# Graph network on one core: masks of the adjacency search made from a bfloat16 copy that the row sums write

## The chip, the cores and the metric

The kernel runs on one core of a Trainium2 chip. The metric is the device time of one launch in microseconds (us), as the median of several runs. One further execution is recorded by the hardware profiler, and every view below is of that one. The engines are named as in the profile: PE is TensorE's matmul (PEld its weight loads), DVE is VectorE, ACT is ScalarE, POOL is GpSimd and SP is the engine that issues most of the DMAs. Each engine works through its own queue in the order of its instructions.

## What is computed

Four graph layers on 2708 nodes with 512 features each; after every layer the old features are added and the sum is normalized (LN). The adjacency matrix `adj` is 2708 x 2708 in float32 and mostly zero; an entry that isn't zero lies between 0.05 and 1.

```python
# layer 0
a = adj + eye;  d = 1 / sqrt(a.sum(axis=1))
x = LN(x + (d[:, None] * a * d[None, :]) @ x @ W0.T + b0)
# layer 1
head = (adj > 0) / max(sqrt(count of adj > 0 in the row), 1e-12);  inc = adj + head
x = LN(x + (inc @ x) / inc.sum(axis=1))
# layer 2: attention over the edges of adj, two gates, a sigmoid
x = LN(x + sigmoid(gate_a * (attn @ (x @ W_sa)) + gate_b * (adj @ (x @ W_g) + b_g)))
# layer 3: signs of x and of a weight
x = LN(x + relu(adj @ (max(sign(x), 0) @ sign(W3).T)))
```

What matters here is layer 0: it needs the sum of every row of `adj` (the degree), and the kernel uses the zeros of the matrix, so it first has to find where the other entries are.

## The kernel before

**The search.** The 2708 rows of `adj` are cut into 22 blocks of 128 (the last has 20). While the blocks stream in from memory, the kernel makes for each a list of the nodes that have an edge into it, so that later only the listed rows of features are gathered and only packed pieces of the matrix are multiplied. Blocks are taken in `GROUPS` of one to three (L55): (1,), (2, 3), (4, 5), (6, 7, 8) and so on up to (21,), and block 0, which is treated as dense, comes last. The order of arrival is in `arrival`.

**Turns.** `turn(at)` (L1242) writes out the work of one turn, and it is called for `at` = 0 to 25. The order is fixed by hand: `in_order` (L620) chains every instruction traced inside it to the one before it on the same engine, DMA issues included. Instructions from outside may be slotted in between by the scheduler. `each(action, k)` does an action for the k-th block to arrive; `chain(action, n)` does it for the group whose last block arrived n turns ago. The second group, called `SOON`, runs its whole chain in one turn, and so does the first group in turn 0.

**The steps that the change and the prediction touch:**

- `load` (L711) brings the block's rows as two halves, 1408 and 1300 columns wide, into buffers `arow`, of which there are four: two blocks. `load_x` brings the block's features and its piece of columns 0 to 127. SP issues both for the block two turns ahead.
- `sum_rows` (L805) is ScalarE's row sum: a copy of each half with an accumulated sum into `row_sums`. The copy itself goes to a buffer `unused` of one byte an element, and nothing reads it.
- `degree` (L813, DVE) adds the two half sums and 1. `root` (L824, ACT) takes the square root. `inverse_root` (L831) makes `dinv` from it by a reciprocal and a Newton step, four small DVE instructions that are placed between the masks.
- `mark` (L850) makes the mask of the block: per half a DVE comparison "not equal to 0" from `arow` into a bfloat16 tile (L874). For a block that lists its own diagonal tile apart, two short instructions follow on `arow` itself: the mask of the own 128 columns (L880) and a read of the diagonal (L886). They lie in the first half for blocks up to 10 and in the second from block 11. Between these stand the `others`: `own_diagonal` (L900) of the block before, `count` (L914) where a group has just become complete, and the four Newton steps. Then 22 small matmuls, `find` (L895), count the entries per node.
- The chain of a group: `count` (DVE) and `count_partitions` (PE) one turn after its last block, `steps_of` (a table on DVE, then the difference matmul L981) and `look_up` two turns after it, with ScalarE's copy `steps` (L990), comparisons on DVE and the `looked` matmuls; `keep_looked` (L1021) is ScalarE's copy of their result in the same turn. `list_nodes` (L1027), three turns after it, makes the list on DVE, and `fetch` (L1070) has POOL issue the indirect DMAs of the packed pieces.
- Feature work goes along: `transpose_x` (PE) for the block of this turn, `keep_transposed` (L1094, ACT) and `project0` (L1101, PE, four float32 matmuls of 512 columns) for the block before, `scale0` (L1111, ACT, with a DMA to `y_rows` from ScalarE's queue) for the one before that, and `fold` (DVE) and `grow0` (PE) for the one three turns back.

In a turn, ScalarE's queue so far has the order root of the block before, row sums of this block, `keep_transposed`, the copy `steps` where a group is at `look_up`, `scale0` with its DMA, and `keep_looked`.

Of the kernel before, what the change touches and what calls it, by code (L numbers as in the profile page):

```python
# [10 lines left out]
BF16 = mybir.dt.bfloat16  # L11
F16 = mybir.dt.float16
I32 = mybir.dt.int32
AF = mybir.ActivationFunctionType
ALU = mybir.AluOpType
# [4 lines left out]
P = 128  # L20
# [487 lines left out]
def sparse_layers(ctx, tc, x, adj, adj_t, w0_t, b0, w_sa, a_sa, w_gcnb, b_gcnb, wa, ba, wb, bb, w3_t,  # L508
# [19 lines left out]
    def rows(b: int) -> int:  # L528
        return min(P, N - b * P)

    def direct(b: int):

        return tuple(range(NB)) if b == 0 else DIRECT.get(b, ())
# [9 lines left out]
    f = [feat.tile([P, D], F32, tag=f"f{b}", name=f"f{b}") for b in range(NB)]  # L543
# [40 lines left out]
    def side_of(b: int):  # L584
        return sides[:, ways.index(SPLIT[b]), :]
# [22 lines left out]
    def own_by_itself(b: int) -> bool:  # L608
        return b not in direct(b)
# [88 lines left out]
    with tc.tile_pool(name="s_pre", bufs=1) as pre:  # L698
# [3 lines left out]
        NT = NB + 3  # L702

        CUT = (NB // 2) * P
        arows = {}
        row_sums = pre.tile([P, NB, 2], F32, name="s_row_sums")

        def place_of_x(b: int):
# [55 lines left out]
        turn_at, at = {}, 0  # L764
# [30 lines left out]
        near = pre.tile([P, KINDS - 1, NB], BF16, name="s_near")  # L795
# [8 lines left out]

        def sum_rows(b: int):  # L805
            m = rows(b)
            for h, ar in enumerate(arows[b]):
                unused = pre.tile([P, CUT], mybir.dt.uint8, tag="unused", name=f"unused{b}_{h}", bufs=1)
                nc.scalar.activation(  # L809
                    unused[:m, : ar.shape[1]], ar, AF.Copy, accum_out=row_sums[:m, b, h : h + 1]  # L810
                )

        def degree(b: int):  # L813

            m = rows(b)
            deg = small.tile([P, 1], F32, tag="deg", name=f"deg{b}")
            nc.vector.scalar_tensor_tensor(  # L817
                deg[:m], row_sums[:m, b, 0:1], 1.0, row_sums[:m, b, 1:2], op0=ALU.add, op1=ALU.add
            )
            degree_of[b] = deg  # L820
# [29 lines left out]
        def mark(b: int, others):  # L850

            others = iter(others)

            def other():
                next(others, lambda: None)()

            g = group_of[b]
            i = g.index(b)  # L860
            m = rows(b)
            if i == 0:
                find = ps_s.tile([P, D], F32, tag="find", name=f"find{b}", bufs=2)
                n = len(g)
                search[g] = {
                    "hits": find[:, : n * NB * KINDS].rearrange(
                        "p (g s c) -> p g s c", g=n, c=KINDS
                    ),
                    "before": find[:, D - n * KINDS :],
                    "diff": find[:, : n * NT * KINDS],  # L870
                }
            mask = masks[arrival.index(b) % 2]
            for ar, c0 in zip(arows[b], (0, CUT)):
                nc.vector.tensor_scalar(  # L874
                    mask[:m, c0 : c0 + ar.shape[1]], ar, 0.0, None, op0=ALU.not_equal
                )
                other()
                own = b * P - c0
                if own_by_itself(b) and 0 <= own < ar.shape[1]:
                    nc.vector.scalar_tensor_tensor(  # L880
                        mask[:m, b * P : b * P + m], ar[:, own : own + m], 0.0, off_dia[:m, :m],
                        op0=ALU.not_equal, op1=ALU.mult,
                    )
                    other()
                    scr = pre.tile([P, P], F32, tag="dia", name=f"dia{b}", bufs=1)
                    nc.vector.scalar_tensor_tensor(  # L886
                        scr[:m, :m], ar[:, own : own + m], 1.0, ident[:m, :m],
                        op0=ALU.mult, op1=ALU.mult, accum_out=dia[:m, b : b + 1],
                    )
            for j in direct(b):  # L890
                nc.vector.memset(mask[:m, j * P : (j + 1) * P], 0.0)  # L891
            for step_ in others:
                step_()
            for s in range(NB):
                nc.tensor.matmul(  # L895
                    search[g]["hits"][:, i, s, :], mask[:m, s * P : (s + 1) * P], side_of(b)[:m],
                    start=True, stop=True,
                )
# [339 lines left out]
        def each(action, at: int):  # L1238
            if 0 <= at < NTURN:
                action(arrival[at])  # L1240

        def turn(at: int):  # L1242
            step_of = {at - last_at[g]: g for g in GROUPS[1:]}

            def chain(action, since: int):
                if step_of.get(since, SOON) != SOON:
                    action(step_of[since])

            each(degree, at - 1)
            each(root, at - 1)  # L1250
            chain(steps_of, 2)
            each(sum_rows, at)
            each(keep_transposed, at - 1)
            steps = inverse_root(arrival[at - 1]) if 0 < at <= NTURN else []
            found_in = step_of.get(1)

            if found_in:
                steps.insert(0, lambda: count(found_in))
            if 0 < at <= NTURN:
                steps.insert(0, lambda: own_diagonal(arrival[at - 1]))  # L1260
            if at < NTURN and arrival[at]:
                mark(arrival[at], steps)
            else:
                for step_ in steps:
                    step_()
            if found_in:
                count_partitions(found_in)
                if found_in == SOON:
                    steps_of(SOON)
            each(load_x, at + 2)  # L1270
            each(load, at + 2)
            each(transpose_x, at)
            chain(look_up, 2)
            chain(list_nodes, 3)
            if found_in == SOON:
                look_up(SOON)
                keep_looked(SOON)
            if at == 0:
                for step_ in (
                    count, count_partitions, steps_of, look_up, keep_looked, list_nodes  # L1280
                ):
                    step_(GROUPS[0])
            each(scale0, at - 2)
            each(project0, at - 1)
            chain(keep_looked, 2)
            each(fold, at - 3)
            each(grow0, at - 3)
            if found_in == SOON:
                list_nodes(SOON)
            fetch(len(to_fetch))  # L1290
            if at == NTURN:
                count_block0()

        with in_order():
            for at in range(NTURN + 4):
                turn(at)
# [84 lines left out]
    with tc.tile_pool(name="s_l0", bufs=10, reuse_waits="tile") as lp:  # L1381
# [77 lines left out]
        for at, b in enumerate(sequence):  # L1459
            m = rows(b)  # L1460
# [108 lines left out]
    with tc.tile_pool(name="s_l1", bufs=8, reuse_waits="tile") as lp:  # L1569
# [67 lines left out]
        for at, b in enumerate(sequence):  # L1637
            m = rows(b)
# [348 lines left out]
    with tc.tile_pool(name="s_l3", bufs=11, reuse_waits="tile") as lp, \  # L1987
# [96 lines left out]
        for at, b in enumerate(order3):  # L2084
            m = rows(b)
# [120 lines left out]
```

## Time and profile before

| | |
|---|---|
| median of 3 runs | 1006.92 us (1006.87 to 1007.9) |
| the profiled execution | 1015.66 us, of which the span of its instructions is 1013.9 us |
| PE busy | 867.5 us (86% of the span) |
| DVE busy | 654.6 us (65%) |
| POOL busy | 513.0 us (51%) |
| ACT busy | 381.2 us (38%) |
| bytes moved | 220.06 MB, on average 217 GB/s |

Times inside the profile are counted from the start of the span. The search takes about the first 190 us of it; layers 0 to 3 fill the rest. The shares in the table are means over all of this, so for a change in the search they say little, and the slices and the timeline of that stretch have to be read. In a row of the groups by line, the numbers after the bar are the busy time in us and the mean of one instruction in ns, and then the engine's idle time before them with what ended it. In a row of the timeline the first number is the start, the second the duration, both in us, and the bracket holds the idle time before it and its releaser. In the list of waits the numbers are the total in us, how many, and the longest.

### The profile page before, as it was taken

Reading aid. Unit: us, or ns where it says so; the run is one execution under the profiler, and the core shown is the slowest. Engines: PE = TensorE matmul, PEld = TensorE weight load, DVE = VectorE, ACT = ScalarE, POOL = GpSimd, SP = SyncE. Lnnn points to the kernel's source line nnn. Section 1 sums busy time; section 2 is a strip of 40 time slices with the busy share of each in tenths; the row PEclk is TensorE's granted clock in tenths of the full one; section 3 lists DMA queues with packets and bytes.
Section 4 is the critical chain, followed back from the end, with each engine's and each line's share of the span. In section 5 each row is a group of like instructions: output and inputs, shape, how many; then the busy total and the mean of one; then the engine's idle time right before and its main releaser. Section 6 shows DMA issues by size and latency. Waiting matters only on the chain.

```text
span 1013.9 us, 12803 instructions
## 1 busy us (share of the span) xinstructions
PE 867.5 (86%) x3659; PEld 458.7 (45%) x3659; DVE 654.6 (65%) x2538; ACT 381.2 (38%) x822; POOL 513.0 (51%) x579
## 2 busy tenths in 40 slices
PE   1888889659587977989999988998999999699983
PEld 0444444212122324455555544453555555378762
DVE  5889797717366863546455436666888777556765
ACT  2665555100000012545445433333444333254654
POOL 2677888567666533646434034453454320066761
PEclk9898889879798988999999998999999999889986
DMA  9999895467676634766645266676786551299985
GB/s 288 332 330 313 293 299 162 142 197 215 189 228 202 199 122 132 216 198 207 199 150 165 80 235 239 225 272 219 261 320 224 176 176 44 82 308 331 310 233 169
DMA packets 93557, 220.06 MB, mean 217 GB/s; under 512 B 13660, under 2 KB 28364, under 8 KB 93476
## 3 DMA queue, kind: packets, MB, share of 16 engines
q0 software_dynamic: 43008, 127.61, 42.1%
q1 hardware_dynamic: 38520, 76.78, 22.3%
q10 hardware_dynamic: 11948, 14.76, 4.4%
q8 instruction: 31, 0.51, 0.2%
q14 instruction: 50, 0.41, 0.1%
HBM read 178.21 MB, written 31.71 MB: 207 GB/s over the span
## 4 chain that ended last, share of the span: by engine, by line
PE 63%; DVE 15%; issue 6%; DMA 6%; another core or an unknown queue 5%; ACT 3%; POOL 1%; ACTq 0%; DVEq 0%; SPq 0%; POOLq 0%
PE l L1369 11%; PE h L1595 7%; PE e L1820 6%; PE a L1820 6%; PE l L2075 4%; PE y L1106 4%; PE pg L1868 4%; PE l L2114 3%; PE pc L1868 3%; DMA xg<-x_rows,i 2%; PE e L1628 2%; PE px L1929 2%; PE a L1629 2%; DVE s_mask L874 1%
## 5 line engine op out<-in xcount | busy, mean ns | idle before, releaser
L613 POOL DMA_INDIRECT xg<-x_rows,i x98 | 94.8, 967 | 113.4 <-PE l L1369 65.7
L1072 POOL DMA_INDIRECT a<-in_adj_t_dram,row_at x98 | 111.0, 1132 | 59.2 <-DVE deg L817 24.0
L613 POOL DMA_INDIRECT xg<-y_rows,i x98 | 97.5, 995 | 50.3 <-issue 21.8
L1106 PE MATMUL y<-s_w,xt 128*128 128x512 f32 (+1 forms) x176 | 96.8, 702 | 0.0
L1369 PE MATMUL l<-xg,a 128*32 128x512 f32 (+3 forms) x196 | 83.2, 657 | 12.1 <-DMA xg<-y_rows,i 11.8
L613 POOL DMA_INDIRECT xg<-xw_rows,i x70 | 71.4, 1020 | 39.9 <-issue 16.5
L1796 POOL DMA_INDIRECT xg<-x_rows,i x60 | 59.9, 999 | 61.8 <-ACT ae L1551 18.0
L1595 PE MATMUL h<-s_wsa,xt 128*128 128x256 f32 (+3 forms) x352 | 83.5, 391 | 5.2 <-ACT xt L1590 5.0
L1796 POOL DMA_INDIRECT a<-x_rows,i x38 | 36.9, 970 | 93.3 <-DVE mask L1554 38.0
L1595 PEld LDWEIGHTS h<-s_wsa,xt 128*128 128x128 f32 (+1 forms) x352 | 65.4, 190 | 30.6 <-ACT xt L1590 14.0
L809 ACT ACTIVATE unused<-arow 128x1408 uint8<-128x1408 f32 (+3 forms) x44 | 58.3, 1325 | 2.4 <-DMA x_rows<-s_zero 1.7
L1106 PEld LDWEIGHTS y<-s_w,xt 128*128 128x128 f32 (+1 forms) x176 | 37.3, 223 | 43.4 <-issue 43.3
L2075 PE MATMUL l<-ws,pw 128*128 128x512 f32 (+1 forms) x210 | 52.0, 401 | 3.7 <-DVE pw L1999 3.7
L1820 PE MATMUL a<-xg,a 128*32 128x512 f32 (+2 forms) x120 | 50.9, 626 | 4.2 <-DMA xg<-x_rows,i 4.2
L1820 PE MATMUL e<-xg,ae 128*32 128x512 f32 (+2 forms) x120 | 47.9, 601 | 0.9 <-ACT ae L1556 0.9
L642 ACT ACTIVATE rsqs<-mv 128x1 f32<-128x1 f32 (+2 forms) x56 | 11.3, 201 | 94.8 <-DVE mv L671 48.9
L2075 PEld LDWEIGHTS l<-ws,pw 128*128 128x128 f32 (+1 forms) x210 | 40.4, 194 | 14.0 <-DVE pw L1999 4.6
L1868 PE MATMUL pg<-s_wg,pt 128*128 128x256 f32 (+1 forms) x176 | 44.9, 397 | 1.3 <-ACT pt L1856 1.3
L895 PE MATMUL find<-s_sides,s_mask 128*128 128x5 bf16 (+1 forms) x462 | 15.7, 166 | 34.8 <-DVE s_mask L891 25.0
L667 DVE BATCH_NORM_STATS2 st<-t 128x6 f32<-128x512 f32 (+1 forms) x66 | 45.3, 686 | 0.3
L1369 PEld LDWEIGHTS l<-xg,a 128*32 128x32 f32 (+3 forms) x196 | 19.6, 148 | 53.2 <-issue 33.0
L673 POOL TENSOR_TENSOR rs<-mv,s_neg_half 128x1 f32<-128x1 f32 (+1 forms) x22 | 12.9, 588 | 60.5 <-DVE mv L671 51.1
(306 smaller groups left out, 1965.6 us busy)
## 6 DMA issues: line engine op xcount, KB each, us to landing
arow<-in_adj_dram SPq DMA_DIRECT2D x21, 704.0 KB
arow<-in_adj_dram SPq DMA_DIRECT2D x21, 650.0 KB
x_rows<-f SPq DMA_DIRECT2D x40, 256.0 KB
aw<-in_adj_t_dram SPq DMA_DIRECT2D x21, 320.0 KB
y_rows<-yt ACTq DMA_DIRECT2D x20, 256.0 KB
x_rows<-h SPq DMA_DIRECT2D x19, 257.0 KB
f<-in_x_dram SPq DMA_DIRECT2D x19, 256.0 KB
h_own<-x_rows SPq DMA_DIRECT2D x19, 256.0 KB
```

The source lines that it names most:

```text
L613: nc.gpsimd.indirect_dma_start(out=t, out_offset=None, in_=src[:, :], in_offset=bass.IndirectOffsetOnAxis(ap=index[b][:, i : i + 1], axis=0),)
L667: nc.vector.bn_stats(st[:m], t[:m])
L809: nc.scalar.activation(unused[:m, : ar.shape[1]], ar, AF.Copy, accum_out=row_sums[:m, b, h : h + 1])
L1072: nc.gpsimd.indirect_dma_start(out=packed[b][:, t + len(direct(b)), :], out_offset=None, in_=adj_t, in_offset=bass.IndirectOffsetOnAxis(ap ...
L1106: nc.tensor.matmul(ps[:m], xt[:, k, :m], w0[:, k, :], start=(k == 0), stop=(k == KC - 1))
L1369: nc.tensor.matmul(ps[r0:r1], weights, moving, start=(i == order[0]), stop=last_of(b, i, order))
L1595: nc.tensor.matmul(ps, xt[:, k, :m], w[:, k, :], start=(k == 0), stop=(k == KC - 1))
L1796: nc.gpsimd.indirect_dma_start(out=g, out_offset=None, in_=x2_rows[:, :], in_offset=bass.IndirectOffsetOnAxis(ap=index[b][:, t : t + 1], a ...
L1820: nc.tensor.matmul(ps[r0:r1], weights, moving, start=(i == order[0]), stop=last_of(b, i, order))
L1868: nc.tensor.matmul(ps, pt[:, k, :m], w[:, k, :], start=(k == 0), stop=(k == KC - 1))
L2075: nc.tensor.matmul(whole[b], p[:r, h, b * P : (b + 1) * P], g[:r, :], start=(j == 0 and h == 0), stop=(j == NB - 1 and h == 1),)
L2114: nc.tensor.matmul(ps[:m], p[:, h, i * m : (i + 1) * m], src[i0 + i], start=False, stop=(i0 + i == len(src) - 1 and h == 1),)
```

## The change

The row sum writes its copy as bfloat16 into two buffers named `rough`, and the masks are made from these instead of from the float32 rows. For that the row sum of a block is moved from the turn of the block to the end of the turn before it; turn 0 does its own first. `degree` moves from the start of the next turn to the end of the block's own turn, and so does `root`, where it stands behind `keep_looked`. The own-diagonal instructions L880 and L886 still read the float32 rows.

```diff
-        arows = {}
+        arows, rough = {}, {}
...
         def sum_rows(b: int):
             m = rows(b)
+            rough[b] = []
             for h, ar in enumerate(arows[b]):
-                unused = pre.tile([P, CUT], mybir.dt.uint8, tag="unused", name=f"unused{b}_{h}", bufs=1)
+                near = pre.tile([P, CUT], BF16, tag="rough", name=f"rough{b}_{h}", bufs=2)
                 nc.scalar.activation(
-                    unused[:m, : ar.shape[1]], ar, AF.Copy, accum_out=row_sums[:m, b, h : h + 1]
-                )
+                    near[:m, : ar.shape[1]], ar, AF.Copy, accum_out=row_sums[:m, b, h : h + 1]
+                )
+                rough[b].append(near[:m, : ar.shape[1]])
...
             mask = masks[arrival.index(b) % 2]
-            for ar, c0 in zip(arows[b], (0, CUT)):
+            for ar, near, c0 in zip(arows[b], rough.pop(b), (0, CUT)):
                 nc.vector.tensor_scalar(
-                    mask[:m, c0 : c0 + ar.shape[1]], ar, 0.0, None, op0=ALU.not_equal
+                    mask[:m, c0 : c0 + ar.shape[1]], near, 0.0, None, op0=ALU.not_equal
                 )
...
-            each(degree, at - 1)
-            each(root, at - 1)
+            if at == 0:
+                each(sum_rows, 0)
             chain(steps_of, 2)
-            each(sum_rows, at)
             each(keep_transposed, at - 1)
...
             each(scale0, at - 2)
             each(project0, at - 1)
+            each(sum_rows, at + 1)
+            each(degree, at)
             chain(keep_looked, 2)
+            each(root, at)
             each(fold, at - 3)
```

## The prediction, made before the changed kernel had run

> **What bounds the kernel now.** The page's slices come first, to see which engines are full while adjacency rows are searched (0 to about 190 us of the span).
>
> ```profile
> DVE  5889797717366863546455436666888777556765
> ACT  2665555100000012545445433333444333254654
> DMA  9999895467676634766645266676786551299985
> ```
>
> One digit is 25.3 us. In slices 2 to 7 DVE is 70 to 90% busy, the DMA engines 80% and more, ScalarE only 50 to 60%: a change that takes work from DVE and gives ScalarE none looks safe. But the share does not say which wait ends last. The groups by line price the two operations concerned, and the list of waits shows what ScalarE idles for:
>
> ```profile
> L809 ACT ACTIVATE unused<-arow 128x1408 uint8<-128x1408 f32 x19 | 25.9, 1362 | 0.0
> L809 ACT ACTIVATE unused<-arow 128x1300 uint8<-128x1300 f32 x19 | 24.5, 1287 | 0.6
> ...
> L874 DVE TENSOR_SCALAR s_mask<-arow 128x1300 bf16<-128x1300 f32 x19 | 17.9, 944 | 0.0
> L874 DVE TENSOR_SCALAR s_mask<-arow 128x1408 bf16<-128x1408 f32 x19 | 17.8, 935 | 0.6 <-DMA arow<-in_adj_dram 0.6
> ...
> ACT steps L990 <- PE find L981: 22.0, 7, 4.9
> ```
>
> The last line decides my forecast: in seven turns ScalarE sits at the head of its queue waiting for a TensorE matmul, 22.0 us together, and whatever stands behind that waits too. The timeline of one cycle of three turns shows where:
>
> ```profile
> 84.30 0.32 PE L981 MATMUL find<-table,s_step 128*128 128x375 bf16 x1
> 84.66 0.47 ACT L990 CAST steps<-find 128x375 bf16<-128x375 f32 x1 [2.69 <-PE find L981]
> 85.03 0.69 ACT L1115 ACTIVATE yt<-y,s_dinv 128x512 f32<-128x512 f32 x1
> 85.75 0.33 ACTq L1116 DMA_DIRECT2D y_rows<-yt  x1
> 86.55 1.00 DVE L874 TENSOR_SCALAR s_mask<-arow 128x1408 bf16<-128x1408 f32 x1
> 87.72 0.83 DVE L874 TENSOR_SCALAR s_mask<-arow 128x1300 bf16<-128x1300 f32 x1
> 90.24 0.53 DVE L1038 TENSOR_TENSOR look<-look,turns 128x352 f32<-128x352 f32 x1
> 93.15 0.89 DVE L874 TENSOR_SCALAR s_mask<-arow 128x1408 bf16<-128x1408 f32 x1
> 99.19 0.43 PE L895 MATMUL find<-s_sides,s_mask 128*128 128x5 bf16 x10 [3.16 <-DVE s_mask L880]
> ```
>
> I call the turns of a group its count turn (count), look turn (steps copy L990) and list turn (list_nodes). Above: the look turn's difference matmul at 84.30, the list turn's masks at 86.55, listing from 90.24, the next count turn's masks from 93.15, and TensorE waiting until 99.19 for that turn's mask. From there TensorE needs 8.15 us (count_partitions, transposes, project0, grow0) to the next difference matmul at 107.34. So the ring is TensorE, then DVE; today DVE enters it without ScalarE, because masks are made straight from the rows.
>
> **What the Trainium skill says.** "VectorE: DVE Perf Modes", the section on the perf-mode tiers: a tensor_scalar from SBUF to SBUF goes at twice the base rate in float32 and four times in bfloat16; its 2048-element figures work out at 150 cycles plus elements over the factor, at 0.96 GHz. For 1408 and 1300 float32 elements that gives 0.89 and 0.83 us, just the undisturbed rows above; for bfloat16, as an estimate, 0.52 and 0.49. No bfloat16 mask is in this trace. "ScalarE: Activation LUTs", What ACT_TABLE_LOAD costs: an ACTIVATE with immediates takes 186 ns plus 0.833 ns per element, float32 and bfloat16 alike: 1.36 us for 1408, and the trace has 1362 ns. So I cost the change of output type on ScalarE at nothing (bounds 0 to 0.1 us). "TensorE: Matmul & The Clock Gate", Part 1: after an idle window the array runs at half clock until busy again; the trace agrees, with single L1106 matmul records from 592 to 1201 ns and a granted clock of 0.72 between 102 and 108 us.
>
> **The change part by part.** (1) Masks from bfloat16: DVE loses 0.94 + 0.94 - 1.01 = 0.87 us a turn, some 18 us over 21 turns. Not all of it is on the path.
>
> (2) The row sum one turn ahead. The mask of turn t+1 now waits for ScalarE's sum, and that stands at the end of turn t, behind the steps copy, scale0 and the y_rows DMA issue on the same queue; the listing copy L1024, the root and the next transposed copy stand behind it. In count and list turns this has cover: ScalarE reaches the sum several us before DVE asks. In the look turn it has none. From the difference matmul: 0.36 until the copy (84.66 - 84.30), 1.45 to the end of the DMA issue (86.1), two halves with their accumulator reads 2.97, a semaphore 0.1, second mask 0.49. The reciprocal then waits for the root, now behind the sum and L1024 (0.49 + 0.2 against the mask's 0.6): 0.3. The rest up to L1038, taken from 88.55 to 90.24 less a 0.35 wait for the sum that goes: 1.35. Together L1038 comes 7.0 us after the difference matmul. Difference starts in the five full cycles: 62.68, 84.30, 107.34, 131.81, 154.99; L1038 before: 68.16, 90.24, 113.94, 137.73, 160.16. So L1038 moves by +1.5, +1.1, +0.4, +1.1, +1.8. The following count turn's two masks get back (measured pair less 1.01) 0.96, 0.95, 1.23, 0.71, 0.67. Net +0.5, +0.1, -0.8, +0.4, +1.1: +1.3 us. The look turns' own saving is worth nothing: DVE then waits for ScalarE, about 2 us at the first mask. The early cycle with the count at 51.5 saves only its second mask, since own_diagonal waits for TensorE until 50.99: -0.4.
>
> (3) The start has no turn ahead. Before:
>
> ```profile
> 5.81 0.89 DVE L874 TENSOR_SCALAR s_mask<-arow 128x1408 bf16<-128x1408 f32 x1 [0.75 <-DMA arow<-in_adj_dram]
> ...
> 11.32 1.02 PE L895 MATMUL find<-s_sides,s_mask 128*128 128x5 bf16 x22 [11.32 <-DVE s_mask L891]
> ...
> 12.33 0.34 ACTq L744 DMA_DIRECT2D x_rows<-s_masked  x1
> ...
> 14.00 1.38 ACT L809 ACTIVATE unused<-arow 128x1408 uint8<-128x1408 f32 x1
> ```
>
> ScalarE issues zero fills until 12.7, loads a table until 14.0, and its halves end at 15.4 and 18.6 (16.9 if the second isn't again held by an interleaved weight load). So the first find moves from 11.3 to 17.6 or 19.2. Before, slack followed: DVE stood 2.92 us for the row sum, ScalarE 2.34 for a DMA. Running the same steps (find to base 4.0, base to look copy about 2.3) the look copy ends at 24.0 or 25.6, the next block's sum at 26.9 or 28.5. Now the root follows with its 1.28 us table load in the open (it ran at 22.0 in a wait before); reciprocal, diagonal and second mask take about 1.2, so the second find starts at 29.6 or 31.2 against 26.40: +3.2 to +4.8, I take +4.0. TensorE is back to back from there to the next find, so nothing absorbs it.
>
> (4) degree and root later: degree is small (0.15 us) and its sum is long done; the root's cost is in (2) and (3). Row buffers come free no later: the half without its own diagonal after the sum, the other after the diagonal read, and SP's x, column and direct-row loads keep their order. ScalarE needs a block earlier than DVE did, but loads are issued about 10 us before use (81.68 for the mask at 93.15) and in list turns the sum would start near 91: bound 0 to 1 us a cycle, taken as 0. The two rough buffers wait for the previous turn's masks, on the same DVE queue, before the sum is due. POOL's fetches shift with the lists: it idles 6.3 us before the last list (183.54), so its backlog doesn't hold it.
>
> **Sum.** +4.0 - 0.4 + 1.3 = about +5 us. Against the profiled execution (1015.66 us, its span 1013.9) that is 1020.6; on the median of 1006.92 it is 1012.
>
> **Rivals.** Faster: DVE is really the bound and the ring through ScalarE loosens. The three DVE turns 79.33 to 99.19 plus 2.3 to the base copy are 22.1 us; less 2.6 they are 19.5. If TensorE, idle less, kept its clock (project0 took 3.68 us for eight matmul records at full clock, 5.85 at 100.8), the 8.15 would shrink to 5.9 and the ring would gain about 2 us a cycle: -10 in five, with +4 at the start -6, so 1001. For: DVE is nearly without gaps from 60 to 107. Against: the wait of 3.16 at 99.19 stays, and with it the slow clock; and DMA, at 0.95 to 1.00 busy from 54 to 108, leaves little room.
>
> No change: the start's loss is half absorbed and the lists gain: 1007.
>
> Much slower: bfloat16 masks run no faster than float32 ones (+0.9 for each list and count turn, +9), or the sums wait for rows in the busy DMA stretches, 1 to 2 us in each cycle: 1018 to 1022. The first half of this is also the case that the change doesn't do what it says; the 16-bit comparisons of L1007 (284 ns for 256 elements, 348 for 512, 0.25 ns an element) speak against it.
>
> **How the numbers follow.** Chances: forecast 0.52, faster rival 0.20, no change 0.12, much slower 0.16. The forecast's own range is 1008 to 1017 (start 3.2 to 4.8, each cycle off by 0.7). For 8 in 10 I go from 1001 to 1020. About 2 us (0.2%) is what can be told from no change. Faster 0.20, within 0.13, slower 0.67.
>
> **What would show it.** Right: masks near 0.5 us; DVE idle at the first mask of list turns with ScalarE's sum as releaser; the first find after 17 us; find-to-difference times still near 8 us. Wrong: cycles under 21 us, or a first find before 14.

## The result, and the profile after

The changed kernel takes 1018.22 us (median of 22 runs, 1010.03 to 1023.26) against 1008.5 us for the kernel before beside it (22 runs). The ratio is 1.0079 with a 95% interval of 1.0056 to 1.0101: 5.6 to 10.2 us slower. The profiled execution took 1022.38 us, its span 1020.4 us. In the changed file the row sum stands one line further down (L809 is L810), what follows it two (L874 is L876, L1038 is L1040), and what follows `turn` up to four.

The slices of the changed kernel, one digit per 25.5 us:

```profile
DVE  4677578727445783555546427766888777555675
DMA  9899797376776625676655257786786551299984
```

DVE has become emptier in the search: slices 2 to 7 have 6 to 8, and one 5, where 7 to 9 stood. The DMA row changes by a tenth or two, both ways. The groups by line, shapes kept apart (busy time and mean ns of one, then the idle time before them by what ended it):

```profile
L810 ACT ACTIVATE rough<-arow 128x1408 bf16<-128x1408 f32 x21 | 28.9, 1377 | 8.4 <-ACT yt L1117 2.2 <-issue 2.1 <-DVE turns L1038 1.0
L876 DVE TENSOR_SCALAR s_mask<-rough 128x1408 bf16<-128x1408 bf16 x20 | 12.0, 598 | 26.2 <-ACT rough L810 16.6 <-issue 9.6
L876 DVE TENSOR_SCALAR s_mask<-rough 128x1300 bf16<-128x1300 bf16 x20 | 10.2, 511 | 2.0 <-ACT rough L810 2.0
```

The masks are as fast as hoped: 598 and 511 ns where 935 and 944 stood, and DVE's busy time fell from 654.6 to 638.2 us. The price is in the last column: 28.2 us of idle time ahead of the masks, 18.6 of them put down to ScalarE's sum; for the other 9.6 the profile names no releaser. The list of waits over the first 200 us has the same 18.6 us, and also what ScalarE itself waits for, TensorE's difference matmul:

```profile
ACT steps L992 <- PE find L983: 24.0, 6, 5.5
...
DVE s_mask L876 <- ACT rough L810: 18.6, 8, 8.0
```

The timeline of the cycle that was shown of before, from the difference matmul of a look turn to the listing of the next turn:

```profile
89.74 0.32 PE L983 MATMUL find<-table,s_step 128*128 128x375 bf16 x1
90.10 0.47 ACT L992 CAST steps<-find 128x375 bf16<-128x375 f32 x1 [4.52 <-issue]
...
91.20 0.33 ACTq L1118 DMA_DIRECT2D y_rows<-yt  x1
91.62 1.38 ACT L810 ACTIVATE rough<-arow 128x1408 bf16<-128x1408 f32 x1 [0.46 <-DMA a<-in_adj_t_dram]
...
93.12 0.53 DVE L876 TENSOR_SCALAR s_mask<-rough 128x1408 bf16<-128x1408 bf16 x1 [3.31 <-ACT rough L810]
94.39 0.50 DVE L876 TENSOR_SCALAR s_mask<-rough 128x1300 bf16<-128x1300 bf16 x1 [0.47 <-ACT rough L810]
96.24 0.53 DVE L1040 TENSOR_TENSOR look<-look,turns 128x352 f32<-128x352 f32 x1
```

Read it downwards: TensorE's matmul, ScalarE's copy of it, the DMA issue, the sum, and only then the mask, for which DVE stood 3.31 us. Listing (L1040) comes 6.50 us after the matmul; before it was 5.94. The chain of waits of the look turn before (start, length, what) runs through the same engines, and shows where it enters ScalarE's queue:

```profile
60.89 5.02 PE y L1108 x8
65.91 0.86 PE l L1136 x2
67.18 0.69 ACT yt L1117
67.91 0.33 ACTq L1118
68.40 1.22 issue
69.62 1.14 ACT rough L810 x2
71.84 0.41 DVE s_mask L876
73.11 0.42 DVE look L1040
```

A row sum, which needs nothing of TensorE, is a link of this chain only because it stands behind the steps copy and scale0 (L1117) in ScalarE's queue (its first half, from 68.33 us, falls into the piece called issue). Something like it happens near the start of the span. The sum for the mask of turn 3 stands at the end of turn 2, behind scale0, which itself has to wait:

```profile
17.32 0.79 PE L897 MATMUL find<-s_sides,s_mask 128*128 128x5 bf16 x22 [17.32 <-DVE s_mask L893]
...
35.31 0.69 ACT L1117 ACTIVATE yt<-y,s_dinv 128x512 f32<-128x512 f32 x1 [2.97 <-issue]
36.47 1.38 ACT L810 ACTIVATE rough<-arow 128x1408 bf16<-128x1408 f32 x1 [0.47 <-issue]
37.97 0.53 DVE L876 TENSOR_SCALAR s_mask<-rough 128x1408 bf16<-128x1408 bf16 x1 [5.05 <-ACT rough L810]
```

The first find comes at 17.32 us instead of 11.32, the second at 28.63 instead of 26.40, the third at 35.10 instead of 32.49, the fourth at 42.77 instead of 38.01. The first gather of layer 0, which ends the search, starts at 210.14 instead of 200.36.

One cycle of this trace, from 111.17 to 138.47, has several microseconds in which PE, DVE and ScalarE stand together, and the profile names no releaser on this core (POOL goes on issuing). The changed kernel was therefore traced again, below, and the sums of times are made from that second trace.

### The profile page after: what moved, and what is told of

It is laid out like the page before. It is cut to its first block, busy times and chain, and to the rows that moved or that the text cites. A ratio compares the mean times of both kernels' runs of the same rounds, so it can differ in the third digit from the quotient of the medians.

```text
span 1020.4 us, 12822 instructions
## 1 busy us (share of the span) xinstructions
PE 865.4 (85%) x3659; PEld 456.4 (45%) x3659; DVE 638.2 (63%) x2538; ACT 380.9 (37%) x822; POOL 500.9 (49%) x579
## 4 chain that ended last, share of the span: by engine, by line
PE 63%; DVE 13%; another core or an unknown queue 7%; issue 6%; DMA 5%; ACT 4%; POOL 0%; ACTq 0%; SPq 0%; DVEq 0%; POOLq 0%
PE l L1373 13%; PE h L1599 7%; PE e L1824 6%; PE a L1824 6%; PE l L2079 5%; PE l L2118 4%; PE pg L1872 3%; PE pc L1872 3%; PE y L1108 2%; DMA xg<-x_rows,i 2%; PE e L1632 2%; PE px L1933 2%; PE a L1633 2%; PE l L1434 2%
## 5 line engine op out<-in xcount | busy, mean ns | idle before, releaser
L1074 POOL DMA_INDIRECT a<-in_adj_t_dram,row_at x98 | 101.5, 1035 | 80.5 <-DVE s_own L1125 23.5
L810 ACT ACTIVATE rough<-arow 128x1408 bf16<-128x1408 f32 (+3 forms) x44 | 58.2, 1324 | 10.1 <-ACT yt L1117 2.2
L2079 PEld LDWEIGHTS l<-ws,pw 128*128 128x128 f32 (+1 forms) x210 | 40.1, 193 | 14.3 <-DVE pw L2003 4.2
L1872 PE MATMUL pc<-s_wg,pt 128*128 128x258 f32 (+1 forms) x176 | 42.1, 381 | 0.0
```

The lines of the kernel that those rows point to most:

```text
L810: nc.scalar.activation(near[:m, : ar.shape[1]], ar, AF.Copy, accum_out=row_sums[:m, b, h : h + 1])
L1074: nc.gpsimd.indirect_dma_start(out=packed[b][:, t + len(direct(b)), :], out_offset=None, in_=adj_t, in_offset=bass.IndirectOffsetOnAxis(ap ...
L1872: nc.tensor.matmul(ps, pt[:, k, :m], w[:, k, :], start=(k == 0), stop=(k == KC - 1))
L2079: nc.tensor.matmul(whole[b], p[:r, h, b * P : (b + 1) * P], g[:r, :], start=(j == 0 and h == 0), stop=(j == NB - 1 and h == 1),)
```

## The experiments

The twelve runs were made in three sets. The kernel before takes 960.49 and 960.72 us in the first two (one chip) and 959.82 us in the third (another), not 1008.5 as in the first comparison, so ratios are compared; 0.1% is one microsecond. Expectations that are given in microseconds were written for a kernel before at 1008 us.

| run | median us | ratio to before | 95% interval |
|---|---|---|---|
| changed kernel again | 968.14 | 1.0076 | 1.0048 to 1.0105 |
| degree and root moved, alone | 959.11 | 0.9991 | 0.9970 to 1.0011 |
| masks from rows, sum last | 955.93 | 0.9942 | 0.9922 to 0.9963 |
| masks from rows, sum ahead | 967.23 | 1.0071 | 1.0052 to 1.0091 |
| first four masks from rows | 962.61 | 1.0025 | 1.0007 to 1.0043 |
| sum early | 949.55 | 0.9881 | 0.9857 to 0.9905 |
| sum early, first four from rows | 951.58 | 0.9906 | 0.9874 to 0.9937 |
| the same, early from turn 4 on | 947.51 | 0.9850 | 0.9824 to 0.9876 |
| the same, early in look turns alone | 956.85 | 0.9953 | 0.9935 to 0.9972 |
| early from 4, four rough buffers | 951.67 | 0.9896 | 0.9852 to 0.9939 |
| early from 4, five row buffers | 947.97 | 0.9873 | 0.9835 to 0.9911 |

**Both kernels again.** No edit.

> The changed kernel once more, on the same chip as the runs beside it, for a trace that can be laid beside theirs. In its first trace one cycle (111 to 124 us) had 6 us in which all engines waited at once. If that stall is a property of the kernel, it comes again at the same place and belongs to the cost of the change; if it is a disturbance of that execution, the cycle is 22 to 24 us as the others are, and the ratio is 1.0079 within its interval either way.

> The kernel before once more, for a trace from the same chip as the other runs. Theory: its search ends (first gather of layer 0) near 194 to 200 us, between the run with the sum last (190) and the changed kernel (204). Rival (the search is as long as in the changed kernel and the difference lies in the layers behind it): 203 us or more.

The stall at 111 us did not come again: the cycle there takes 23.8 us (111.90 to 135.73), so it belonged to that execution. The ratio is the same, and the search of the kernel before ends at 196.22 us, within its theory. DVE's waits for the sum stand out more clearly in this trace, as its masks and the list of waits show:

```profile
38.75 0.53 DVE L876 TENSOR_SCALAR s_mask<-rough 128x1408 bf16<-128x1408 bf16 x1 [6.57 <-ACT rough L810]
...
70.91 0.55 DVE L876 TENSOR_SCALAR s_mask<-rough 128x1408 bf16<-128x1408 bf16 x1 [3.24 <-ACT rough L810]
92.69 0.53 DVE L876 TENSOR_SCALAR s_mask<-rough 128x1408 bf16<-128x1408 bf16 x1 [2.70 <-ACT rough L810]
115.28 0.53 DVE L876 TENSOR_SCALAR s_mask<-rough 128x1408 bf16<-128x1408 bf16 x1 [3.89 <-ACT rough L810]
139.38 0.74 DVE L876 TENSOR_SCALAR s_mask<-rough 128x1408 bf16<-128x1408 bf16 x1 [5.08 <-ACT rough L810]
160.69 1.00 DVE L876 TENSOR_SCALAR s_mask<-rough 128x1408 bf16<-128x1408 bf16 x1 [2.96 <-ACT rough L810]
```
```profile
DVE s_mask L876 <- ACT rough L810: 36.9, 13, 8.1
```

The last five of these masks are those of the five list turns. The search of this trace ends at 204.07 us, 7.85 us after that of the kernel before, where the medians differ by 7.4 and the two profiled executions by 6.6. So the search holds the whole loss. It divides at the difference matmul of the first full cycle:

| from these traces, us | before | changed | |
|---|---|---|---|
| third difference matmul (the start) | 61.70 | 67.68 | +6.0 |
| from it to L1040, five cycles | 27.12 | 32.80 | +5.7 |
| from L1040 to the next difference matmul, five cycles | 82.87 | 79.30 | -3.6 |
| from the eighth difference matmul to the first gather | 24.53 | 24.29 | -0.2 |

These parts are of one trace each, from different chips, and single traces scatter. In the first pair of traces the start is +3.9 us (66.60 against 62.68). The next run below takes as long as the kernel before, and yet its trace has the third difference matmul at 59.68 and the end of the search at 192.29 us, 2.0 and 3.9 us sooner than the one used here. A part of the table is therefore sure to some 2 us, no better.

**Degree and root alone**, in the kernel before:

```diff
-            each(degree, at - 1)
-            each(root, at - 1)
             chain(steps_of, 2)
...
+            each(degree, at)
             chain(keep_looked, 2)
+            each(root, at)
```

> The kernel before with one part of the change alone: degree and root stand at the end of the block's own turn instead of at the start of the next one. Nothing is written as bfloat16, the sum stays in its turn. On DVE degree then stands ahead of fold, and the root, which in the kernel before waited 32 us in 13 cases for degree and fold, comes sooner, and so does the next block's sum behind it. Theory (this is the gain of 0.6% that the run with the sum last showed): ratio 0.992 to 0.997. Rival (that gain came from the bfloat16 output or the second buffer): 0.998 to 1.002.

This was meant to explain the gain of the next run below, and the theory fell: 0.9991, no change. Degree's position is worth nothing by itself.

**Masks from the rows, the sum last.** The changed kernel with `ar` in place of `near` in the mask, and the sum of the next block behind the listing copy and the root:

```diff
-                    mask[:m, c0 : c0 + ar.shape[1]], near, 0.0, None, op0=ALU.not_equal
+                    mask[:m, c0 : c0 + ar.shape[1]], ar, 0.0, None, op0=ALU.not_equal
...
-            each(sum_rows, at + 1)
             each(degree, at)
             chain(keep_looked, 2)
             each(root, at)
+            each(sum_rows, at + 1)
```

> As the run with masks from the float32 rows, but the row sum of the next block stands last on ScalarE's turn, behind the listing copy and the root: ScalarE's order is then that of the kernel before, and what is left of the change is the bfloat16 output, two buffers for it, and the place of degree on DVE. Theory (the 0.7% that the run with float32 masks lost come from the sum standing ahead of the listing copy and the root in look turns): ratio to the kernel before 0.998 to 1.002, L1040 about 6 us or less after the difference matmul. Rival (the bfloat16 output or its wait for a free buffer costs): it stays at 1.005 to 1.009.

It is faster than the kernel before, by 0.4 to 0.8%, which neither theory had. Its trace points to one cause at the start. In the kernel before, two loads of layer 3's weights (L1411) stand on ScalarE's queue inside turn 0, and ScalarE stands still around them; in this run and in the changed kernel they are issued after 180 us. First the timeline of ScalarE in the run with degree and root alone, which still has them:

```profile
16.52 0.35 ACTq L1411 DMA_DIRECT2D s_w<-in_w_t_dram  x1
16.92 1.29 ACT L809 ACTIVATE unused<-arow 128x1300 uint8<-128x1300 f32 x1 [1.42 <-DMA x_rows<-s_zero]
...
20.43 0.34 ACTq L1411 DMA_DIRECT2D s_w<-in_w_t_dram  x1
20.81 0.27 ACT L990 CAST steps<-find 128x125 bf16<-128x125 f32 x1 [2.51 <-DMA x_rows<-s_masked]
```

and of the run with the sum last:

```profile
15.34 1.27 ACT L810 ACTIVATE rough<-arow 128x1300 bf16<-128x1300 f32 x1
...
17.62 0.27 ACT L992 CAST steps<-find 128x125 bf16<-128x125 f32 x1 [0.91 <-PE find L983]
18.49 0.33 ACT L1026 COPY look<-looked 128x200 f32<-128x200 f32 x1 [0.61 <-PE looked L1016]
18.84 1.28 ACT L830 ACT_TABLE_LOAD   x1
```

The steps copy comes 3.2 us sooner and the second find 3.0 us sooner (23.24 against 26.28). So some 3 us of the gain look like a side effect: the loads have moved. No run moved these loads alone. Why they move is read from the order of the built programs, not from a run. In a build of the kernel before in which only the sum's output is made two bfloat16 buffers, they leave turn 0 as well; with one bfloat16 buffer, or two of one byte, they stay. Two buffers of 2816 bytes a partition, where one of 1408 stood, thus seem to leave the weights no room so early. The other 2 us of the 0.5% between these two runs, which were on different chips, stay open.

**Masks from the rows, the sum ahead.** Only the first edit of the former run: the sum stands where the change put it, ahead of listing copy and root, and nothing reads `rough`.

> The changed kernel with the masks made from the float32 rows again; the bfloat16 copy is still written one turn ahead and read by nobody, and degree and root stay at the end of a turn. Theory (ScalarE's order is part of the cost, since the root stands behind the sum in list turns): the start's 4 to 6 us come back, the masks cost 0.87 us more a turn on DVE, the reciprocal of list turns now waits for the root instead of the mask waiting for the sum, so L1040 stays near 6.5 us after the difference matmul: 1010 to 1015 us. Rival A (the masks' wait on ScalarE alone makes the cost): back at the kernel before, 1006 to 1010. Rival B (DVE is what bounds the cycle, and the bfloat16 masks were a gain): above 1020.

1.0071, at the upper end of the theory's range; neither rival. Against the run with the sum last, the sum's position alone costs 1.3%, 11 to 12 us, although no mask waits for it. In the traces (one each), the third difference matmul comes 4.35 us later (61.21 against 56.86), and the five cycles after it are 5.8 us longer (115.00 against 109.22). At the start the reason stands in ScalarE's timeline:

```profile
18.67 0.33 ACT L1026 COPY look<-looked 128x200 f32<-128x200 f32 x1 [0.60 <-PE looked L1016]
21.90 1.38 ACT L810 ACTIVATE rough<-arow 128x1408 bf16<-128x1408 f32 x1 [2.90 <-DMA arow<-in_adj_dram]
...
24.90 1.28 ACT L830 ACT_TABLE_LOAD   x1
```

The sum of block two waits for its rows, and the root of block one with its table load behind it: 24.90 instead of 18.84. In the cycles, two other instructions of DVE wait in place of the masks:

```profile
89.00 0.16 DVE L1144 TENSOR_TENSOR s_row_sum<-s_row_sums 128x3 f32<-128x3 f32 x1 [1.16 <-ACT rough L810]
...
89.48 0.16 DVE L659 RECIPROCAL root<-root 128x1 f32<-128x1 f32 x1 [0.32 <-ACT root L830]
```

`s_row_sum` adds the halves of its own group's sums, of blocks that came turns before, but it stands until the newest sum has ended: 9.5 us in the five cycles. The reciprocal then waits 0.2 to 0.3 us more for the root, which stands behind that sum too, and this wait ends last. L1040 comes 6.46 us after the difference matmul, mean of the five cycles, where it comes 5.47 us after it with the sum last.

**The first four masks from the rows**, all others from the bfloat16 copy:

```diff
-                    mask[:m, c0 : c0 + ar.shape[1]], near, 0.0, None, op0=ALU.not_equal
+                    mask[:m, c0 : c0 + ar.shape[1]], ar if arrival.index(b) < 4 else near, 0.0, None, op0=ALU.not_equal
```

> The changed kernel with the masks of the first four blocks (turns 0 to 3, the start, where no turn ahead exists) made from the float32 rows, all others from the bfloat16 copy. Theory: the first find is back at about 11.3 us, the fourth at about 38 instead of 42.8, and the 4 to 5 us of the start stay recovered to the end: 1012 to 1015 us. Rival (the start is absorbed later, by the DMA or by the ring): the first finds come earlier but the difference matmul at 185 us and the end don't move, 1017 to 1020.

The ratio of 1.0025 is below that of the theory's range (1012 to 1015 are 1.004 to 1.007), but the gain on the changed kernel beside it, 0.5% or 5 us, is what the theory gave the start (4 to 5 us). The fourth find is at 39.74 and the third difference matmul at 61.13, 6.55 us sooner than in the changed kernel. Beside the former run it also weighs the bfloat16 masks of the other turns: the ratio falls by 0.46%, and the five cycles from 115.00 to 110.38 us. (The changed kernel, with the same code in these cycles, has 112.10.)

**The sum early**: ahead of `look_up`, so that it stands before the steps copy, scale0 and the y_rows DMA on ScalarE.

```diff
+            each(sum_rows, at + 1)
             chain(look_up, 2)
...
             each(project0, at - 1)
-            each(sum_rows, at + 1)
             each(degree, at)
```

> The changed kernel with one line moved: the row sum of the next block stands ahead of the look turn's steps copy, scale0 and the y_rows DMA on ScalarE instead of behind them. Masks stay bfloat16, the start stays as changed. Theory (ScalarE's queue order: the sum waits for TensorE's difference matmul through the steps copy): DVE's wait of about 3.3 us at the first mask of list turns goes, L1040 comes about 4.5 to 5 us after the difference matmul instead of 6.5, each of five to six cycles is about 2 us shorter, so 1006 to 1010 us. Rival A (the rows are then needed earlier than they land): the sum waits for DMA and holds the steps copy behind it, 1018 or more. Rival B (the loss lies in the start or outside the search): no change, 1016 to 1020.

0.9881: one moved line turns a loss of 0.8% into a gain of 1.2%. That is below the theory's range (1006 to 1010 are 0.998 to 1.002), with about twice the gain that it gave. Rival A's wait is there (the sum waits for rows 19.4 us in 17 cases), but not its price.

**Early, and the first four from the rows**: both edits.

> Both of the two former edits: the sum ahead of the steps copy, and the masks of the first four blocks from the float32 rows. Theory: both losses go and DVE's 0.87 us a turn is left as a gain on the ring, so below the kernel before: 998 to 1006 us. Rival A (early sums wait for rows): 1012 or more. Rival B (the ring is set by TensorE or DMA once the wait is gone, so a faster mask gains nothing): equal to the kernel before within 2 us.

0.9906 lies in the theory's range, but no better than the early sum alone, so the start's 5 us are lost again. ScalarE's timeline in turn 0 tells where:

```profile
21.28 1.38 ACT L810 ACTIVATE rough<-arow 128x1408 bf16<-128x1408 f32 x1 [4.26 <-DMA arow<-in_adj_dram]
...
22.88 1.29 ACT L810 ACTIVATE rough<-arow 128x1300 bf16<-128x1300 f32 x1
...
24.16 0.25 ACT L992 CAST steps<-find 128x125 bf16<-128x125 f32 x1
```

The difference matmul was at 17.63; the steps copy stood 6.5 us behind a sum whose rows had not landed.

**Early from turn 4 on**, and **early in look turns alone**. Both keep the first four masks from the rows. The condition, `at > 3` in the first and `at > 3 and step_of.get(2)` in the second:

```diff
+            if at > 3:
+                each(sum_rows, at + 1)
             chain(look_up, 2)
...
-            each(sum_rows, at + 1)
+            if not (at > 3):
+                each(sum_rows, at + 1)
```

> As the run with both edits (first four masks from the rows, sum ahead of the steps copy), but the sum stands early only from turn 4 on; in turns 0 to 3 it stands at the end of the turn as in the changed kernel. In the run with both edits the steps copy of turn 0 stood 6.5 us behind a sum that waited for the second block's rows, and the gain of the start was lost. Theory (that wait is what ate the start's gain): the first difference matmul at about 17.5 us is followed by its steps copy at once, the second find is back at about 27 us instead of 29.6, and the ratio falls from 0.990 to 0.984 to 0.987. Rival (from turn 4 on arrival of the rows sets the pace, so an earlier start only waits longer): 0.988 to 0.992.

> As the run with the sum early from turn 4 on, but early only in look turns; in count and list turns it stands at the end as in the changed kernel. Theory (the loss sits in look turns alone, where the sum stood behind a copy that waits for TensorE; in the other turns the early sum buys nothing and only waits for rows): equal to or up to 0.4% better than the run with the early sum in all turns from 4, ratio 0.982 to 0.987. Rival (the rows' arrival sets the pace in all turns): the same within 0.2%. Second rival (the early sum in count and list turns also helped, as masks came sooner): worse, 0.990 to 0.998.

From turn 4 on: 0.9850, as the theory said; no mask of the search waits for a sum any more. It is 1.5% faster than the kernel before and 2.2% faster than the changed one (its interval overlaps that of the early sum alone). In look turns alone: 0.9953, so the second rival holds. Both start from the run with the first four masks from the rows, at 1.0025: the early place in look turns is worth 0.7% of the 1.7%. The sum needs an early place in the other turns too, once the ring is shorter. The timeline of ScalarE and DVE in a list turn of that run shows how:

```profile
87.93 0.69 ACT L1117 ACTIVATE yt<-y,s_dinv 128x512 f32<-128x512 f32 x1 [3.81 <-PE y L1108]
...
89.07 1.38 ACT L810 ACTIVATE rough<-arow 128x1408 bf16<-128x1408 f32 x1 [0.46 <-DMA a<-in_adj_t_dram]
...
90.57 0.53 DVE L876 TENSOR_SCALAR s_mask<-rough 128x1408 bf16<-128x1408 bf16 x1 [2.54 <-ACT rough L810]
```

scale0 waits for project0 on TensorE, and the sum and the count turn's mask behind it.

Why is the gain so large? The busy times between the third and the eighth difference matmul, that is the five cycles, first of the kernel before, then of the changed one, then with the sum early from turn 4 on (length, busy time and instructions of PE, PEld, DVE, ACT and POOL, granted TensorE clock, DMA share, GB/s):

```profile
61.70:171.69 109.99, 95.76 (x620) 51.87 (x619) 96.67 (x374) 63.63 (x115) 91.21 (x100) 0.89 0.88 291
```
```profile
67.68:179.78 112.10, 97.45 (x621) 52.21 (x620) 84.62 (x366) 63.47 (x115) 82.70 (x100) 0.88 0.86 280
```
```profile
60.92:156.57 95.65, 86.87 (x620) 46.75 (x619) 85.77 (x371) 63.23 (x113) 78.47 (x95) 0.98 0.94 330
```

The same 620 matmul records take 86.87 us instead of 95.76, at a granted clock of 0.98 instead of 0.89: 8.9 of the 14.3 us. TensorE's idle time (length less busy time) falls from 14.2 to 8.8 us: the other 5.4. These are single traces again: the run with both edits, which has the same code in the five cycles, takes 99.62 us there at 0.93. "TensorE: Matmul & The Clock Gate", Part 1 of the Trainium skill, has the array at half clock after an idle window; that fits in the main. All traces with 12.6 us or more of idle time in this stretch have a clock of 0.87 to 0.91, and all with 6.8 to 11.6 us have 0.93 to 0.98. But the sum of the idle time alone does not order them: the run with the early sum alone has 0.95 with 6.8 us. No run set the clock apart from the idle time.

**More buffers** for the best of these: `rough` with `bufs=4`, and `arow` with `bufs=5`.

> As the run with the sum early from turn 4 on, with four rough buffers instead of two. There the sum waited 5.2 us in five cases for a mask to free its buffer, and the steps copy stood behind. Theory (these waits are on the ring): 2 to 5 us less, ratio 0.980 to 0.984. Rival (the rows arrive no sooner, so the sum only waits for the DMA instead): within 0.2% of that run, 0.983 to 0.987.

> As the run with the sum early from turn 4 on, with five buffers for half rows instead of four, so that one half's load is issued sooner. There the sum waited 14.8 us in 17 cases for rows. Theory (the rows' arrival is what bounds the early sum, and it is set by when a buffer is free): ratio 0.978 to 0.983. Rival (the DMA engines are full, busy 0.9 and more while the search streams, so an earlier issue lands no earlier): 0.983 to 0.987.

Neither is a gain: 0.9896 and 0.9873, and neither reaches its theory's range (nor, quite, its rival's; both ran on the other chip than the run with two rough buffers). The lists of waits give one reason. The sum's waits for rows, with two rough buffers,

```profile
ACT rough L810 <- DMA arow<-in_adj_dram: 14.8, 17, 3.3
```

become, with four of them,

```profile
ACT rough L810 <- DMA arow<-in_adj_dram: 21.1, 23, 2.6
```

and, with five row buffers, 18.5 us in 17 cases. The 5.2 us that the sum had waited for a free rough buffer are gone with four; it waits for its rows instead. That the medians are higher by 0.2 to 0.5% is within the intervals and stays unexplained.

A second reason lies on an engine that was off the path. With two rough buffers, early from turn 4 on, these are POOL's last wait above 0.5 us and the first gather of layer 0:

```profile
88.36 1.47 POOL L1074 DMA_INDIRECT a<-in_adj_t_dram,row_at  x1 [2.75 <-DVE s_own L1125]
...
182.64 0.94 POOL L613 DMA_INDIRECT xg<-y_rows,i  x1 [0.30 <-issue]
```

Between them POOL issues 65 fetches of packed pieces and never waits longer than 0.5 us, 1.45 us for each on the mean, and the gather stands behind them in its queue. In the kernel before POOL still waited 6.29 us for the last list. With four rough buffers the eighth difference matmul comes 1.9 us sooner (154.72 against 156.57), but POOL is as full and the gather comes 1.8 us later. So in these two traces POOL's issues, and no longer the ring, set the end of the search. The trace with five row buffers is another case: there the five cycles took 101.29 us, and POOL waited 3.68 us for the last list.

Not tried: fewer or cheaper fetches on POOL; an `s_row_sum` that does not wait for the newest sum; and the root ahead of the sum in turns 0 to 3 on top of the best version, whose second find is at 27.85 where the run with the sum last has it at 23.24.

## Why the prediction was right, and where it was not

The forecast was +5 us, slower, with 1001 to 1020. Measured was +9.7 us in the medians, +5.6 to +10.2 by the interval. Sign and range hold; the forecast's size is just below the interval, and the median lies above the narrower 1008 to 1017 that the sum was given.

- **Step 1, the masks.** The estimate from the Trainium skill ("VectorE: DVE Perf Modes", the perf-mode tiers) was 0.52 and 0.49 us; undisturbed ones take 0.53 and 0.50. DVE's busy time fell by 16.4 us, where 18 stood. That little of this reaches the path holds too.
- **Step 2, the ring through ScalarE.** The mechanism is as told: DVE idle at the first mask of list turns, the sum as releaser. L1040 moves by +5.7 us over five cycles, where +5.9 stood; the following part gains 3.6, where 4.5 stood; the cycles together +2.1 instead of +1.3. The first agreement is in part luck: the delay after the matmul is 6.5 us, not 7.0, but the second trace of the kernel before has 5.4, where the trace that the step used had 5.8. Of the 0.5 that 7.0 is too long, 0.2 lie in the step's own sum, as 0.49 + 0.2 - 0.6 is 0.1 and not 0.3. The wait itself is mis-sized: 2.7 to 5.1 us instead of about 2. And one reading is wrong: DVE did not enter the ring without ScalarE before. Its `s_row_sum`, just ahead of L1038, waited for the newest sum there too, 0.35, 1.45 and 1.45 us in three of the five list turns; the step has the 0.35 alone. The run with masks from the rows shows what this and the root behind the sum come to: five cycles 5.8 us longer than with the sum last, with no mask waiting.
- **"In count and list turns this has cover: ScalarE reaches the sum several us before DVE asks."** In the five full cycles of the changed kernel this holds: all 19.1 us that masks wait for a sum there fall to masks of list turns, whose sum stands in the look turn. But it is no rule. The sum stands behind scale0 in every turn, and scale0 can wait for project0 on TensorE. The prediction had nothing for turns 2 and 4, which are neither count, look nor list turns: the masks behind them, of turns 3 and 5, waited 6.57 and 2.01 us in the second trace. And in the run with the sum early in look turns alone, whose ring is shorter, the cover is gone in a list turn as well.
- **Step 3, the start.** The term of the sum that was most mis-sized: +3.6 with the early cycle, measured +6.0 in the second pair of traces (+3.9 in the first) and some 5 us by the medians, as the run with the first four masks from the rows gave back. The first find at 17.3 is right. But the +4.0 was expected at the second find, with nothing to absorb it. There only +1.0 arrived by the second pair of traces (+2.2 by the first), chiefly, it seems, because the weight loads that held ScalarE in turn 0 were gone, a case that the step left open for the sum but not for the steps copy. The rest came later: +3.25 at the fourth find, +6.0 at the third difference matmul, with the waits of turns 3 and 5 named above. Taking the first four masks from the rows brought 6.55 us back at that place. That the loads moved is in part luck for the forecast: without it the start would have lost more.
- **Step 4, degree and root.** Nothing, as costed: 0.9991 for their place alone. Late rows, taken as 0 to 1 us a cycle, hold back no sum in the five cycles of the second trace by its list of waits; in turn 0 they matter, as the root stood behind a sum that waited 2.90 us in the run with masks from the rows. The DMA row was read too high: it has 8 and 9 in slices 2 to 6, but 5 in slice 7.
- **The rivals.** The faster one was wrong for this change: the ring did not loosen and the clock stayed at 0.88. But its mechanism is real. Once the sum stood early (from turn 4 on), the time from the last find of a count turn to the next difference matmul fell to 5.1 to 5.7 us (from 6.8 to 8.5 in the second trace of the changed kernel), near the 5.9 that the rival gave. "Much slower" was wrong in both causes, though its 1018 is the number that came.

## What to carry to other kernels

When an operation becomes the source of something on the path, look at everything that already stands ahead of it in its queue, in every kind of turn, and ask what each of those waits for: the queue hands their waits on. A producer that needs nothing from an engine should stand ahead of the instructions that do, but not ahead of others while its own data is still on the way. Look also at what is read along with the data that is needed: an addition of old row sums stood here for the newest one. A few microseconds of TensorE's idle time taken out of a ring can pay twice: in these traces the granted clock was higher too. And when a ring gets faster, ask which engine off the path fills up next; here it was POOL.

## What the runs showed of the hardware

- In the best run, 5.4 us less of TensorE's idle time in 110 us went with a granted clock of 0.98 instead of 0.89, and with 8.9 us less for the same matmuls. Over all traces, 12.6 us of idle time or more went with 0.87 to 0.91, and 6.8 to 11.6 us with 0.93 to 0.98.
- With POOL's queue full, an indirect DMA of a packed piece took 1.45 us of it on the mean (65 in 94.3 us).
- With one output buffer of one-byte elements the second half of a row sum most often starts 1.48 to 1.49 us after the first, with two of bfloat16 1.36 to 1.38 us (kernel before and changed kernel). In the kernel before nobody reads the buffer. No run set the number of buffers apart from the type.
- After scale0's DMA issue on ScalarE's queue the row sum starts 0.40 to 0.50 us behind the end of scale0 in 18 of 19 turns in each of the changed kernel's two traces; the issue itself is 0.33 to 0.36 us of it.
- The kernel before takes 1008.5 us in the first comparison and 960 us on the two chips of the experiments, with a mean granted clock of 0.924 in its first trace and 0.952 in its second; the search ends at 200.36 and 196.22 us there, so nearly all of the difference lies behind it. Ratios carried over: 1.0079 and 1.0076 for the changed kernel.
- The stall of PE, DVE and ScalarE near 111 us in the first trace of the changed kernel did not come again, and its cause is open.
